# Two-layer graph network on one core: keys from seven block products, squares in two halves at the end of the aggregate, statistics a slot later

## Chip, core and metric

The kernel runs on one core of a Trainium2 chip. The metric is the device time of one launch in microseconds; lower is better. The core has five engines that run side by side and are held together by semaphores: TensorE (PE, matrix products; its weight loads are listed as PEld), VectorE (DVE), ScalarE (ACT), GpSimd (POOL) and SyncE (SP, which here only issues transfers). Transfers are carried by 16 DMA engines. Products land in PSUM, in banks of 128 x 512 numbers; everything else lives in SBUF. All numbers are float32.

## What is computed

There are B = 16 graphs of N = 1024 nodes with C = 256 features, one weighted adjacency matrix for all, and two layers, each with a layer norm and a relu in front and a residual behind:

```python
h = jnp.maximum(_layernorm(x, axis=-1), 0.0)
x = x + L0(h)          # attention, queries from the graph
h = jnp.maximum(_layernorm(x, axis=-1), 0.0)
x = x + L1(h)          # graph convolution, two dense layers with batch norm

# L0
fea = jnp.transpose(x, (0, 2, 1))
c_adj = jnp.mean(fea, axis=1)
diff = c_adj[:, None, :] - c_adj[:, :, None]
A = jnp.abs(jnp.abs(jax.nn.sigmoid(diff) - 0.5) - 0.5) * 2.0
A_s = (A + jnp.transpose(A, (0, 2, 1))) * 0.5
Wg = adj[None, :, :] * A_s
g = jax.nn.relu(jnp.einsum('bcn,bnm->bcm', fea, Wg) * para.reshape(1, C, N))
q = ...                                   # g, split into 4 heads of 64
kv = (x @ kv_w) ...                       # keys and values, 4 heads each
attn = jax.nn.softmax(jnp.einsum('bhnd,bhmd->bhnm', q, k) * scale, axis=-1)
out = jnp.einsum('bhnm,bhmd->bhnd', attn, v)

# L1
deg = row sums + column sums - diagonal of (adj + I)
A_hat = A_norm * dinv[:, None] * dinv[None, :]
agg = jnp.einsum('nm,bmd->bnd', A_hat, features)
h = jax.nn.relu(_batchnorm(agg.reshape(-1, d) @ W1.T + b1, g1, be1))
out = _batchnorm(h @ W2.T + b2, g2, be2)
```

The batch norms of L1 run over all graphs and nodes, so that the kernel has two stages: everything up to the first dense layer, graph by graph (`layers`), and then the second dense layer (`second`), which the change leaves alone.

## The kernel before

**The loop.** `attention` (L1215) walks 16 graphs x 4 units x 4 = 256 steps. A unit is one pair of heads and one half of the queries. In each step TensorE makes two score tiles (`scores`, L1056; ScalarE takes the exponential into a tile `p`, L1064) and two products of the earlier step's `p` with the values (L1099). VectorE adds the `p` tiles up for the softmax's denominators (L1085, L1088). The tiles `p` have four buffers.

**The background.** Between the scores and the next step, the step takes work from a generator `background(b)`, which holds all other products: each piece is worth some microseconds (`yield 1.71` for two products, `yield 0.86` for one), and a step takes pieces until the sum is at `due`, which grows evenly to `total` over a graph's 16 steps (L1231 to L1236). Instructions are issued to each engine in just the order in which this Python code makes them, and engines work their own list from front to back. `soon(action)` puts an action off to the beginning of the next piece; `weave(main, (start, side), ...)` takes one piece of each side along with each piece of main from number `start` on.

In the background of graph b stand, in this order:
- four pieces of `keys_values(b+1)`: the keys (L670). Each key block of 128 x 512 is the sum of two products of a weight block of `kvw` with a block of the transposed features `ht`: eight products, copied out of PSUM by ScalarE (L681);
- `queries(b+1)`, 7 x 4 products instead of 8 x 4, by the same way of combining quarters (Strassen and Winograd's) that the change now uses for the keys. VectorE weighs adjacency tiles for it (`weigh`, L493) and combines them (`take`, L569);
- the other four pieces of `keys_values(b+1)`, the values, with the second half of `normed(b-1)`, the layer norm for layer 1;
- `aggregate(b-1)`: 7 x 4 products (`pa`), in 14 pieces; from the fourth piece on `summed(b+2)` goes along, the first layer norm of graph b+2 and `differences(b+2)`, which sends the node means through HBM to every partition (`cbc`);
- `prepare(b+2, hidden(b-1))`: the 14 products of the first dense layer (`py`), with `squares(b+2)` after the second product and `gathered(b+2, k)` after the seventh and the tenth.

Graph 0 has a background of its own, with `plain_queries(1)`, the adjacency's combination for the aggregates (`graph`) and the degrees.

**Squares.** The transposed features `ht` come by way of HBM: `squares` (L432) turns 32 x 32 blocks on VectorE into one tile `sq` of 1 MB (tag `h`, a pool with two buffers) and GpSimd issues one transfer to `hsq_d`; `gathered` brings it back in the other order, in four transfers for each half, issued by SP.

```python
sq = p2.tile([P, CC, N], F32, tag="h", name=f"sq_{b}")
for k in range(CC):
    nc.vector.transpose(...)
nc.gpsimd.dma_start(out=hsq_d[b], in_=sq)
```

**Banks.** `bank(name)` hands out the three PSUM banks of the pool `ps_mm` in turn, to `pg`, `pk`, `pv`, `pa`, `py` and `sums` alike: a product can start when the third one before it in this series has been emptied.

**Hidden.** In `hidden` (L795) seven products a half give four blocks, `m1` to `m7`. `m1` and `m5` are emptied by ScalarE (L831, L851), the others by additions on VectorE: `m2` L837, `m3` L842, `m4` L847, `m6` L860, `m7` L866. `put` (L822) has GpSimd send the block to HBM (L824) and puts the batch norm's statistics of the block (L825, VectorE) off with one `soon`. The order of products is m1, m5, m6, m2, m3, m7, m4 in the first half and m1, m6, m2, m5, m7, m3, m4 in the second.

**Other lines.** `steps_of` (L780): the differences of the aggregate's blocks (L786, L787 on VectorE, L788 on GpSimd). L727 and L744: the aggregate's last additions and scaling. `fold` (L1134, L1135): a unit's denominators. `load_later` (L303): loads `w1`, makes its combinations on GpSimd and spreads `dinv` over the partitions.

Of the kernel before, what the change touches and what calls it, by code (L numbers as in the profile page):

```python
# [10 lines left out]
F32 = mybir.dt.float32  # L11
# [6 lines left out]
P = 128  # L18
# [5 lines left out]
def gnn_two_layers_kernel(  # L24
# [12 lines left out]
    nc = tc.nc  # L37
    B, N, C = x.shape
# [60 lines left out]
    def layers(shifted):  # L99
# [31 lines left out]
        def soon(action):  # L131

            queue.append(action)
# [169 lines left out]
        def load_later():  # L303
            later["w1"] = big.tile([P, CC, H1], F32, tag="w1", name="w1")
            nc.sync.dma_start(out=later["w1"], in_=w1_t.rearrange("(k p) j -> p k j", p=P))
            later["s"] = big.tile([P, 4, H1 // 2], F32, name="w1s")
            s1, s2, s3, s4 = (later["s"][:, i] for i in range(4))
            a11, a12, a21, a22 = w1_quarters()
# [123 lines left out]
        def squares(b):  # L432

            sq = p2.tile([P, CC, N], F32, tag="h", name=f"sq_{b}")
            for k in range(CC):
                nc.vector.transpose(
                    sq[:, k].rearrange("p (i t s) -> p i t s", i=NS, s=SQ),
                    hs["a", b][:, :, k * P : (k + 1) * P].rearrange("p t (i s) -> p i t s", s=SQ),  # L440
                )
            nc.gpsimd.dma_start(out=hsq_d[b], in_=sq)

        def gathered(b, k):

# [222 lines left out]
                        yield 1.71  # L668

        def keys_values(b):  # L670
            ht = hts[b]
            ks[b] = [p4.tile([P, N], F32, tag="k", name=f"k_{b}_{k}") for k in range(CC)]
            for g in range(NH):
                for j in range(CC):
                    cols = slice(g * FB, (g + 1) * FB)
                    pk = bank(f"pk_{b}_{j}_{g}")
                    for k in range(CC):
                        product(
                            pk, kvw[:, k, j * P : (j + 1) * P], ht[k][:, cols], k == 0, k == CC - 1
                        )  # L680
                    nc.scalar.copy(ks[b][j][:, cols], pk)  # L681
                    yield 1.71

            vs[b] = [p4.tile([P, NT, P], F32, tag="v", name=f"v_{b}_{k}") for k in range(CC)]
            for g in range(NT // 2):
                pv = bank(f"pv_{b}_{g}").rearrange("p (j c) -> p j c", j=2)
# [10 lines left out]
                for k in range(CC):  # L697
                    nc.scalar.copy(
                        vs[b][k][:, 2 * g : 2 * g + 2, :], pv[:, :, k * P : (k + 1) * P]
                    )  # L700
                yield 1.71

        def aggregate(b):
# [91 lines left out]
        def hidden(b):  # L795
# [26 lines left out]
            def put(y, n, j):  # L822
                i = b * NH + n
                nc.gpsimd.dma_start(out=y1_d[i][:, j, :], in_=y)  # L824
                soon(lambda: nc.vector.bn_stats(stats1[:, j, i, :], y))  # L825

            add = nc.vector.tensor_add

# [97 lines left out]
        def summed(b):  # L926
            yield from Norm(b, True).all()
            differences(b)
            yield 0.0

        def prepare(b, products):


            w = weighers[b]
            yield from islice(products, 1)
            yield from islice(products, 1)
            squares(b)
            yield from weave(islice(products, 5), (0, islice(w, 2)))
            gathered(b, 0)
            yield from weave(islice(products, 3), (0, islice(w, 1)))  # L940
            gathered(b, 1)
            yield from weave(islice(products, 3), (0, islice(w, AHEAD - 3)))
            yield from products
# [3 lines left out]
        def background(b):  # L947

            if b == 0:
                differences(1)  # L950
                for k in range(CC):
# [263 lines left out]
        def attention():  # L1215
# [7 lines left out]
            for s in range(len(steps) + 2):  # L1223
                if s < len(steps):
                    unit, g = steps[s]
                    b = unit.at[0]
                    if s % per_graph == 0:
# [460 lines left out]
```

## Time and profile before

| what | us |
| --- | --- |
| median of 3 runs (lowest, highest) | 2484.15 (2481.71, 2485.78) |
| the profiled execution | 2482.2 |
| its span in the trace | 2480.3 |
| first score product | 54.1 |
| start of graph 1, 2, 3 | 164.9, 303.7, 439.9 |
| each of the graphs 3 to 13 | 135.47 or 135.48 |
| graph 14 | 122.2 |
| last graph from | 2052.3 |

Times in the text are microseconds from the beginning of the span. From the beginning of the last graph 428 us are left, of which the second stage has the larger part. In the lists of waits a line gives the engine that stood, the tile and line that it was about to do, what released it, then the sum of the waits, their number and the longest. In timelines a line gives start, duration, engine, line, operation, tiles out and in, and sizes.

### The profile page before, as it was taken

The page shows a single profiled execution, that of the slowest core. Times are in us where ns is not written, and L with a number is a line of the kernel's source. Part 1 is how long each engine was busy: PE and PEld are TensorE (multiplying, and loading weights), DVE is VectorE, ACT ScalarE, POOL GpSimd, SP SyncE. Part 2 cuts the span into 40 slices and gives each one's busy share as a digit, 9 for nine tenths or more (in the row PEclk, how much of TensorE's full clock was granted, in tenths as well). Part 3 has the DMA queues.
Part 4 walks back from the last instruction along what each step waited for, and adds up shares of the span by engine and source line. Part 5 has one row for each costly group of instructions (what it writes and reads, how often), then busy time and mean ns, then how long its engine had stood idle before and what let it go on. Part 6 is the DMA issues. An engine that isn't in the chain of part 4 may idle for free. (4 is left out here: it accounts for less than half of the span.)

```text
span 2480.3 us, 35952 instructions
## 1 busy us (share of the span) xinstructions
PE 2418.3 (97%) x13290; PEld 829.3 (33%) x13290; DVE 1999.8 (81%) x3103; ACT 1261.2 (51%) x1870; POOL 565.2 (23%) x632
## 2 busy tenths in 40 slices
PE   9999999999999999999999999999999999999995
PEld 4333232332323232323323232323233232334444
DVE  5678887979798888889797978888897978767775
ACT  7764454545463645545454645355454534345554
POOL 1480202112121202021111212120201102136652
PEclk9999999999999999999999999999999999999997
DMA  4665535354555544453545555544535453456559
GB/s 145 198 218 175 181 124 191 120 198 157 181 174 191 168 168 162 144 181 118 210 143 175 170 191 170 187 160 148 177 126 197 133 199 122 157 205 222 192 198 373
DMA packets 202682, 437.19 MB, mean 176 GB/s; under 512 B 21248, under 2 KB 96512, under 8 KB 196736
## 3 DMA queue, kind: packets, MB, share of 16 engines
q1 hardware_dynamic: 173328, 327.29, 39.9%
q0 software_dynamic: 29168, 107.50, 11.4%
q8 instruction: 107, 1.75, 0.3%
q14 instruction: 79, 0.65, 0.1%
HBM read 331.36 MB, written 103.35 MB: 175 GB/s over the span
## 5 line engine op out<-in xcount | busy, mean ns | idle before, releaser
L1064 ACT ACTIVATE p<-sc 128x1024 f32<-128x1024 f32 x512 | 495.6, 1020 | 581.4 <-PE sc L1056 579.7
L1088 DVE TENSOR_TENSOR acc<-acc,p 128x1024 f32<-128x1024 f32 x384 | 469.5, 1223 | 81.6 <-ACT p L1064 60.3
L1056 PE MATMUL sc<-q,k 64*64 64x512 f32 x4096 | 500.1, 603 | 4.2 <-ACT p L1064 4.2
L1099 PE MATMUL o<-p,v 128*64 128x512 f32 x2048 | 494.6, 604 | 0.0
L174 PE MATMUL pa<-aht,h_b 128*64 128x512 f32 x1536 | 346.0, 592 | 1.1 <-ACT h_b L368 1.1
L174 PE MATMUL pg<-w,x_h 128*64 128x512 f32 x1472 | 332.0, 592 | 1.9 <-DVE x_h L579 1.9
L1056 PEld LDWEIGHTS sc<-q,k 64*64 64x64 f32 x4096 | 131.7, 132 | 340.9 <-issue 287.8
L1117 POOL DMA_DIRECT2D out_d<-os x58 | 33.9, 584 | 914.9 <-DVE os L1113 883.9
L1099 PEld LDWEIGHTS o<-p,v 128*64 128x64 f32 x2048 | 124.4, 136 | 297.9 <-issue 272.4
L493 DVE SCALAR_TENSOR_TENSOR w<-w,adj 128x1024 f32<-128x1024 f32 x128 | 166.2, 1306 | 31.9 <-ACT w L514 26.1
L174 PEld LDWEIGHTS pa<-aht,h_b 128*64 128x64 f32 x1536 | 110.0, 137 | 220.7 <-issue 208.8
L174 PEld LDWEIGHTS pg<-w,x_h 128*64 128x64 f32 x1472 | 105.6, 137 | 212.4 <-issue 201.0
L506 ACT ACTIVATE w<-cbc,csum 128x512 f32<-128x512 f32 x256 | 170.3, 716 | 4.7 <-DMA cbc<-csum_d 4.7
L514 ACT ACTIVATE w<-w 128x1024 f32<-128x1024 f32 x128 | 135.5, 1059 | 2.5
L569 DVE TENSOR_TENSOR w<-w,w 128x1024 f32<-128x1024 f32 x112 | 133.2, 1219 | 1.5
L174 PE MATMUL py<-at,w1s 128*64 128x512 f32 x448 | 109.5, 598 | 9.7 <-DVE y L837 7.5
L174 PE MATMUL pv<-kvw_f,ht 128*64 128x256 f32 x1024 | 116.1, 379 | 0.0
L174 PE MATMUL pk<-ht,kvw_f 128*64 128x512 f32 x512 | 115.2, 592 | 0.2 <-ACT ht L430 0.2
L174 PE MATMUL py<-at,w 128*64 128x512 f32 x464 | 113.3, 595 | 1.3 <-DVE at L727 0.7
L368 ACT ACTIVATE x_h<-x_h,lnsm_a 128x256 f32<-128x256 f32 x120 | 70.5, 593 | 74.6 <-DMA aht<-aht_d 67.1
L1085 DVE TENSOR_TENSOR acc<-p,p 128x1024 f32<-128x1024 f32 x64 | 79.2, 1237 | 31.5 <-ACT p L1064 31.5
L1428 ACT ACTIVATE yin_f<-yin_f,sm_f 128x512 f32<-128x512 f32 x128 | 93.5, 802 | 15.0 <-DMA yin_f<-y_d 14.9
(197 smaller groups left out, 2967.1 us busy)
## 6 DMA issues: line engine op xcount, KB each, us to landing
aht<-aht_d SPq DMA_DIRECT2D x224, 512.0 KB
adj<-in_adj_dram SPq DMA_DIRECT2D x128, 512.0 KB
y_d<-y POOLq DMA_DIRECT2D x128, 256.0 KB, 3.8
yin_f<-y_d SPq DMA_DIRECT2D x32, 1024.0 KB
para<-in_para_dram SPq DMA_DIRECT2D x64, 256.0 KB
x_d<-x_x POOLq DMA_DIRECT2D x16, 1024.0 KB, 5.1
xo_f<-x_d SPq DMA_DIRECT2D x32, 512.0 KB
out_dram<-xo_f POOLq DMA_DIRECT2D x32, 512.0 KB, 11.1
```

The lines of the kernel that those rows point to most:

```text
L174: nc.tensor.matmul(dst[r], left[:, r], right, start=start, stop=stop)
L368: nc.scalar.activation(self.h[:, t, :], self.src[:, t, :], AF.Relu, bias=self.sm[:, 1, t : t + 1], scale=self.sm[:, 0, t : t + 1], accum_o ...
L493: nc.vector.scalar_tensor_tensor(w, w, 1.0, a, op0=ALU.add, op1=ALU.mult)
L506: nc.scalar.activation(w[:, t, :].rearrange("p (t q) -> p t q", q=P), cbc[:, q * NT // NH : (q + 1) * NT // NH], AF.Abs, bias=csum[:, th * ...
L514: nc.scalar.activation(made[i], made[i], AF.Tanh, scale=-0.5 / C)
L569: nc.vector.tensor_sub(block(i)[part], block(x)[part], block(y)[part])
L1056: nc.tensor.matmul(sc[part, e, :], ks[b][k][r, m * P + c * HW : m * P + (c + 1) * HW], qs[b][k][r, f * FB : (f + 1) * FB], start=True, sto ...
L1064: nc.scalar.activation(pr, sc, AF.Exp)
L1085: nc.vector.tensor_add(self.acc, self.held, pr)
L1088: nc.vector.tensor_add(self.acc, self.acc, pr)
L1099: nc.tensor.matmul(self.o[r, :], vs[b][k][:, m, r], pr[:, e, :], start=(m == 0), stop=(m == NT - 1),)
L1428: nc.scalar.activation(y, y, AF.Relu, bias=sh[:, j : j + 1], scale=scale[:, j : j + 1])
```

## The change

The diff, without the parts that only move lines; `key_steps`, `keys_of` and `values_of` are new.

```diff
@@ load_later
+            later["kvs"] = kvs = p1.tile([P, 4, P], F32, tag="kvs", name=f"kvs_{kind}")
+            combined(kvs, key_weights())
             later["s"] = big.tile([P, 4, H1 // 2], F32, name="w1s")
+            combined(later["s"], w1_quarters())
@@ squares
-            sq = p2.tile([P, CC, N], F32, tag="h", name=f"sq_{b}")
             for k in range(CC):
+                sq = p1.tile([P, N], F32, tag="sq", name=f"sq_{b}_{k}")
                 nc.vector.transpose(
...
-            nc.gpsimd.dma_start(out=hsq_d[b], in_=sq)
+                nc.gpsimd.dma_start(out=hsq_d[b][:, k], in_=sq)
+                yield 0.0
@@ keys_values
+            if b > 2:
+                yield from values_of(b)
+                yield from keys_of(b)
+                return
...
+        def key_steps(b):
+            b11, b12, _, b22 = blocks(hts[b])
+            two = p1.tile([P, N], F32, tag="sq", name=f"kt_{b}")
+            t1, t2 = steps[b] = two[:, :FB], two[:, FB:]
+            nc.vector.tensor_sub(t1, b12, b11)
+            nc.vector.tensor_sub(t2, b22, t1)
+
+        def keys_of(b):
...
+            def second(m):
+                add(c11, m, c12)
+                sub(b21, b21, t2)
+
+            def fifth(m):
+                add(c21, m, c12)
+                nc.gpsimd.tensor_add(c12, c12, c22)
+                nc.gpsimd.tensor_add(c22, c22, c21)
+
+            for i, (left, right, after) in enumerate(
+                (
+                    (a11, b11, lambda m: nc.scalar.copy(c12, m)),
+                    (a12, b21, second),
+                    (s1, t1, lambda m: nc.scalar.copy(c22, m)),
+                    (s2, t2, lambda m: add(c12, m, c12)),
+                    (s3, b12, fifth),
+                    (s4, b22, lambda m: add(c12, m, c12)),
+                    (a22, b21, lambda m: add(c21, m, c21)),
+                )
+            ):
+                made = bank(f"pk_{b}_{i}")
+                product(made, left, right, True, True)
+                after(made)
+                yield 0.86
+
+        def values_of(b):
+            ht = hts[b]
+            if b > 2:
+                key_steps(b)
...
+                if b > 2 and g == NT // 2 - 1:
+                    _, b12, _, b22 = blocks(ht)
+                    soon(lambda: nc.vector.tensor_sub(b12, b22, b12))
@@ hidden, put
-                soon(lambda: nc.vector.bn_stats(stats1[:, j, i, :], y))
+                soon(lambda: soon(lambda: nc.vector.bn_stats(stats1[:, j, i, :], y)))
@@ summed
             differences(b)
             yield 0.0
+            yield from squares(b)
@@ prepare
-            squares(b)
-            yield from weave(islice(products, 5), (0, islice(w, 2)))
             gathered(b, 0)
+            yield from weave(islice(products, 6), (0, islice(w, 2)))
@@ background, graph 0
-                yield from weave(
-                    plain_queries(1), (0, w), (4, norm), (5, graph()), (7, degrees())
-                )
+                asked, build, sums = plain_queries(1), graph(), degrees()
+                yield from weave(
+                    islice(asked, 13),
+                    (0, w),
+                    (4, norm),
+                    (5, islice(build, 8)),
+                    (7, islice(sums, 6)),
+                )
                 differences(2)
+                yield from weave(asked, (0, build), (0, sums))
@@ background, the others
                 yield from weave(islice(products, 4), (0, islice(w, 4)))
+                yield from weave(queries(b + 1), (0, double(w)), (9, islice(norm, 5)))
                 if b == 1:
                     load_later()
-                yield from weave(queries(b + 1), (0, double(w)), (9, islice(norm, 5)))
@@ attention
-                        total -= 10.3 * (b == B - 1)
+                        total -= 10.3 * (b == B - 1) + 0.8 * (1 < b < B - 1)
```

`combined` holds the four combinations (s1 = a21 + a22, s2 = s1 - a11, s3 = a11 - a21, s4 = a12 - s2) that stood in `load_later`. In what is computed nothing changes but the order of additions in the keys of graphs 3 to 15. For these graphs the values now come first, in the place of the keys, and the keys follow behind the queries. The pool p1 has one buffer for each tag, so that the two halves of `sq` and the keys' two differences take turns in one buffer of 512 KB.

More of the change, by code (lines that the diff above doesn't have):

```diff
@@ L305, in load_later, with combined @@
             nc.sync.dma_start(out=later["w1"], in_=w1_t.rearrange("(k p) j -> p k j", p=P))
+            later["kvs"] = kvs = p1.tile([P, 4, P], F32, tag="kvs", name=f"kvs_{kind}")
+            combined(kvs, key_weights())
             later["s"] = big.tile([P, 4, H1 // 2], F32, name="w1s")
-            s1, s2, s3, s4 = (later["s"][:, i] for i in range(4))
-            a11, a12, a21, a22 = w1_quarters()
+            combined(later["s"], w1_quarters())
+        def combined(into, quarters):
+            s1, s2, s3, s4 = (into[:, i] for i in range(4))
+            a11, a12, a21, a22 = quarters
             nc.gpsimd.tensor_add(s1, a21, a22)
@@ L432, in squares @@
         def squares(b):
-            sq = p2.tile([P, CC, N], F32, tag="h", name=f"sq_{b}")
             for k in range(CC):
+                sq = p1.tile([P, N], F32, tag="sq", name=f"sq_{b}_{k}")
                 nc.vector.transpose(
-                    sq[:, k].rearrange("p (i t s) -> p i t s", i=NS, s=SQ),
+                    sq.rearrange("p (i t s) -> p i t s", i=NS, s=SQ),
                     hs["a", b][:, :, k * P : (k + 1) * P].rearrange("p t (i s) -> p i t s", s=SQ),
                 )
-            nc.gpsimd.dma_start(out=hsq_d[b], in_=sq)
+                nc.gpsimd.dma_start(out=hsq_d[b][:, k], in_=sq)
+                yield 0.0
         def gathered(b, k):
@@ L682, in keys_values, with blocks, key_weights @@
                     yield 1.71
+            yield from values_of(b)
+        def blocks(pair):
+            return [pair[k][:, g * FB : (g + 1) * FB] for k in range(CC) for g in range(NH)]
+        def key_weights():
+            return [kvw[:, k, j * P : (j + 1) * P] for j in range(CC) for k in range(CC)]
+        def key_steps(b):
[5 more added lines that the diff above has]
+        def keys_of(b):
+            ks[b] = [p4.tile([P, N], F32, tag="k", name=f"k_{b}_{k}") for k in range(CC)]
+            a11, a12, _, a22 = key_weights()
+            s1, s2, s3, s4 = (later["kvs"][:, i] for i in range(4))
+            b11, b12, b21, b22 = blocks(hts[b])
+            c11, c12, c21, c22 = blocks(ks[b])
+            t1, t2 = steps.pop(b)
+            add, sub = nc.vector.tensor_add, nc.vector.tensor_sub
+            def second(m):
[24 more added lines that the diff above has]
+                key_steps(b)
             vs[b] = [p4.tile([P, NT, P], F32, tag="v", name=f"v_{b}_{k}") for k in range(CC)]
```

## The prediction

> **What bounds the kernel now.** I read the page first, then the table of windows over the whole span, then who waits for whom on TensorE, then one graph in the middle (graph 8, 1117.24 to 1252.71 us) engine by engine. The chain that ended last tells little here: it is cut at 2210 us, in the second layer's normalisation, which the change doesn't touch.
>
> ```profile
> span 2480.3 us, 35952 instructions
> ...
> PE 2418.3 (97%) x13290; PEld 829.3 (33%) x13290; DVE 1999.8 (81%) x3103; ACT 1261.2 (51%) x1870; POOL 565.2 (23%) x632
> ```
>
> TensorE is busy for 97% of the span. Busy is modelled, so I checked the pace: in the timeline one 128x128 by 128x512 product follows the next after 0.86 us (31.76 to 32.62), at a granted clock of 1.00, and from graph 3 to 13 every graph takes 135.47 us. What TensorE waits for in the whole middle (210 to 2050 us):
>
> ```profile
> PE py L174 <- DVE y L837: 7.5, 13, 0.6
> PE py L174 <- DVE y_sum L866: 2.2, 13, 0.2
> PE py L174 <- DVE y L842: 0.5, 1, 0.5
> ```
>
> So 0.74 us a graph, all in the hidden products, whose three PSUM banks VectorE must empty. And before that, in the beginning (60 to 210 us):
>
> ```profile
> PE sc L1056 <- ACT p L1064: 3.7, 1, 3.7
> PE pg L174 <- DVE x_h L579: 1.9, 1, 1.9
> ```
>
> A graph has 16 steps (two score tiles, two value products, some background). VectorE, by step of graph 8 (columns: length, PE, PEld, DVE, ACT, POOL, clock, DMA share, GB/s), shown for steps 5, 7, 12, 13 and 14:
>
> ```profile
> 1160.12:1169.01 8.89, 8.89 (x50) 2.71 (x49) 8.75 (x15) 1.94 (x2) 0.28 (x1) 1.00 0.41 145
> ...
> 1176.20:1185.12 8.92, 8.92 (x74) 4.44 (x72) 5.59 (x8) 6.79 (x15) 0.00 (x0) 1.00 0.95 343
> ...
> 1219.22:1226.40 7.18, 7.18 (x43) 2.15 (x41) 5.00 (x9) 1.94 (x2) 0.62 (x1) 1.00 0.09 36
> 1226.40:1235.29 8.89, 8.89 (x50) 2.72 (x48) 8.18 (x10) 4.22 (x6) 3.00 (x2) 1.00 0.56 174
> 1235.29:1243.77 8.48, 8.31 (x47) 2.26 (x45) 8.24 (x12) 4.24 (x6) 3.82 (x5) 1.00 0.64 221
> ...
> sum 135.47, PE 134.73 PEld 43.17 DVE 115.35 ACT 68.44 POOL 23.32; mean PE 8.42 PEld 2.70 DVE 7.21 ACT 4.28 POOL 1.46
> ```
>
> VectorE is full in steps 13 to 15 and 3 to 6, and has room in 7 to 12. Its late point is step 14:
>
> ```profile
> 1226.98 0.69 DVE L787 TENSOR_TENSOR at<-at,at 128x512 f32<-128x512 f32 x1
> 1227.59 0.70 DVE L1134 STREAM_TRANSPOSE acc<-acc 128x512 f32<-128x512 f32 x1
> ...
> 1233.31 2.37 DVE L438 STREAM_TRANSPOSE sq<-x_h 128x1024 f32<-128x1024 f32 x2
> ...
> 1238.31 2.54 DVE L1088 TENSOR_TENSOR acc<-acc,p 128x1024 f32<-128x1024 f32 x2
> 1240.77 0.69 DVE L842 TENSOR_TENSOR y<-py,y 128x512 f32<-128x512 f32 x1
> ```
>
> L842 (m3) empties a bank that m1 of the second half, three products on, needs; that product is due at 1241.73, the bank is free at 1241.46. So VectorE may be 0.3 us later here before TensorE stands. Behind L842, L866 (m7) must end by 1242.59 for the product after; it ends at 1242.70, and that is the 0.17 us of the list above.
>
> **What the Trainium skill says.** "PSUM — Partial Sum Buffer", "Engine vs sequencer instructions": VectorE's and GpSimd's queues are strictly first in, first out. The trace agrees: VectorE stood 4.75 us for an adj load at 191.7 with nothing passing it. "DMA: Bandwidth & Descriptors", "Anatomy of one DMA": a GpSimd transfer costs some 2.0 us plus bytes/436 GB/s until its semaphore fires. The trace: out_d, 256 KB, 2.4 us (page's rule 2.6); hsq_d, 1 MB, 4.2 at least and 5.0 in the median (rule 4.4). It agrees where nothing else is in flight.
>
> **The change part by part.** Times are graph 8's, with 11 dropped (28.81 is 1228.81); the order is that of the changed program's instructions on each engine.
>
> *One product less.* Keys of graphs 3 to 15 take 7 products in place of 8: 13 x 0.86 = -11.2 us. ACT loses two copies (0.585 us each) a graph, which nothing waits for.
>
> *The keys' differences.* VectorE gets nine operations of 0.69 us: two in step 0, one in step 1, two in step 6, four in step 7. Steps 1 and 2 have 2.0 us of VectorE's idling (0.16, 0.39, 1.47), which hides nearly all of the 2.1 us there. In steps 6 and 7 I walked VectorE's new order: the sums of step 7 are due at 80.75 instead of 79.49, end at 83.2, and the add that empties the fourth key bank ends at 83.9, while the seventh product wants that bank at 83.49. Stall: 0.45 us (bounds 0 and 0.9, as ScalarE's eight value copies at 0.377 in steps 0 and 1 replace four of 0.585). The following add waits for GpSimd (c12+c22; like operations took 1.29 to 1.71 us), twice, some 2.5 us; that falls into the 5.3 us that VectorE stood at 81 to 87 and reaches no one.
>
> *Squares.* The two transposes (1.22 us each) leave step 13 for step 12, and go from one buffer of 1 MB in p2 to a single buffer of 512 KB in p1, used twice. So the second transpose waits until the first one's transfer has landed; the built program has this wait on VectorE. In graphs 2 to 13 the order there becomes: L787, first square, the two at-operations of the seventh aggregate product, second square, fold, the sums of step 13, two hidden adds, fold, the sums of step 14, L842. Walk: first square ends at 28.81; GpSimd is free then (its b12 subtraction runs 27.10 to 28.81) and issues at 29.05; VectorE stands before the second square at 30.09. With a landing time L it goes on at 29.05+L+0.05, a hole h = L-0.99. Nothing behind it idles, so h arrives whole at L842's successor: without a hole it would end at 40.92, with one at 40.92+h, and TensorE needs it at 41.73. TensorE's stall there is h-0.76 instead of 0.17. In step 15 the same lag makes the old 0.57 into 0.68. Together h-0.82 more than before.
>
> L is not shown for 512 KB. From below: the rule's 2.0+1.2 = 3.2 us (an estimate; between out_d's 2.4 and hsq_d's 4.2 the line gives 3.0). From above: 5.0, the median of the whole 1 MB. The broadcast of cbc (512 KB, issued at 28.70) flows in the same microseconds; I take 4.0. Then h = 3.0 and the cost is 2.2 us a graph (1.4 to 3.2).
>
> In graph 1 a step's border stands between the two squares, fold and sums fill the hole: nothing lost, perhaps 0.4 us won. Graph 14 has no squares: it keeps its 0.86.
>
> *Statistics one slot later.* The 0.69 us of L825 go behind L866 and L842, which is in the walk above; without the hole this and the earlier squares would end the 0.17 and most of the 0.57.
>
> *Loads.* gathered(b,0) is issued earlier, so SP stands for its landing ahead of two adj loads; their first user (w in step 14) is 8 us later. gathered(b,1) comes one product later, 10 us before its first reader. Neither is on the path.
>
> *The beginning.* differences(2) goes three background slots ahead: the cbc load that ScalarE stood 4.7 us for at 143.6 lands earlier, and TensorE's 3.7 goes. load_later moves behind the queries: SP stood from 173.6 to 188.0 over w1 and dinv ahead of the adj loads, VectorE 4.75 and TensorE 1.9. Both go: -5.7 us (0 to -5.7). What load_later now delays (aht for 240 us, dbc) has 10 us. What is late next is not seen.
>
> *Sum.* Graphs 2 to 13: -0.86+0.45+2.2 = +1.8, times 12 = +21.5. Graph 14 -0.9, graph 1 -0.4, beginning -5.7. In all +14.5. The profiled execution took 2482.2 us (span 2480.3), so 2496.7; its median is 2484.15, 2.0 above, so **2498**.
>
> **The rivals.**
> - *The wait is covered* (faster). L is 2.2 us or less, as out_d's 2.4 nearly is, or the copy out is let go earlier than I think. Then 13 products (-11.2), the beginning (-5.7), 0.45 x 12 = +5.4 and some -0.3 x 12 = -4: 2469. For: without other traffic small transfers land fast. Against: the skill's 3.2 and hsq_d's own minimum. The point at which the whole change turns is L = 2.8: 12 x (L-2.22) = 7.0. Chance 0.18.
> - *It comes out even.* L between 2.6 and 3.0, or no stall among the keys and L near 3.2: 2484. For: the estimate's low end is close by. Against: cbc's transfer. 0.11.
> - *VectorE becomes the bound* (slower still). It goes from 115.35 to 121.6 us of some 135, 90%; if a third of the 6.2 reaches TensorE on top of the hole, 12 x 2.1 = +25: 2523. For: L842's margin of 0.3 us. Against: 20 us idle a graph, most of it just behind the keys. 0.07.
> - *The forecast*, the hole in steps 12 to 15: its own range 2487 (L 3.2, no key stall) to 2511 (L 5). 0.64.
>
> **How the numbers follow.** A difference of 0.2%, 5 us, is what can be told from no change. Slower: 0.64 x 0.97 + 0.07 = 0.69; the even case and a rest of the forecast give same 0.12; faster 0.19. The range of 8 in 10 goes from 2472, well into the faster case, to 2513.
>
> **What would show it.** Right: VectorE idle 2 to 4 us before the second sq transpose in graphs 2 to 13, ended by hsq_d's landing; TensorE waiting 1.5 to 3.5 us in py for the add of L842; graphs 2 to 13 at some 137.3 us. The keys: a wait of 0 to 0.9 us in pk. The beginning: no gap over 1 us between 140 and 210. Wrong: a graph of 134 us, hsq_d landing under 2.8 us, or fold standing between the squares in the trace.

## The result and the profile after

The changed kernel took 2587.98 us (median of 4 runs, 2584.95 to 2594.78) beside 2483.32 us of the kernel before (4 runs, 2481.71 to 2485.78): ratio 1.0424, 95% interval 1.0404 to 1.0443. It is slower, as forecast, but by 105 us, not by 14. The page of its profiled execution begins:

```profile
span 2586.0 us, 36047 instructions
...
PE 2438.8 (94%) x13238; PEld 827.1 (32%) x13238; DVE 2080.3 (80%) x3220; ACT 1244.1 (48%) x1844; POOL 599.7 (23%) x675
```

TensorE has 52 matmul records fewer (13 products of four) and is "busy" 20 us longer, and its share fell from 97% to 94%. So two things happened: it stood more, and it was slower while it was busy. What it stood for from graph 1 to 14 (210 to 2140 us; columns: sum, number, longest):

```profile
PE py L174 <- DVE y L913: 37.9, 13, 3.2
PE pa L174 <- DMA aht<-aht_d: 20.4, 1, 20.4
PE pk L174 <- ACT k L735: 15.4, 12, 1.3
PE py L174 <- DVE y L931: 10.8, 11, 1.6
PE pk L174 <- DVE k L723: 8.3, 12, 1.1
PE pk L174 <- DVE k L736: 5.8, 8, 0.7
PE py L174 <- DVE y L908: 1.8, 2, 1.2
```

L913, L931 and L908 are the hidden additions that were L842, L860 and L837 before. Three groups stand here: one wait of 20.4 us for the aggregate's first block, some 2.5 us a graph among the keys (pk), some 4 us a graph in the hidden products (py). Between 60 and 210 us the same list is empty: the 3.7 and 1.9 us of the beginning are gone.

By the first score product of each graph, and over graphs 2 to 13 (mean of a graph, from the trace; "half clock" is the time with a granted clock of 0.5, which costs half of itself):

| us | before | after |
| --- | --- | --- |
| graph 0 | 110.8 | 105.5 |
| graph 1 | 138.8 | 160.0 |
| graphs 2 to 13, each | 135.53 | 143.02 |
| of it TensorE idle in py / pk | 0.79 / 0 | 4.07 / 2.46 |
| of it half clock | 0 | 4.27 |
| graph 14 | 122.23 | 121.93 |

The 105.7 us between the spans are thus -5.2 in graph 0, +21.2 in graph 1, +89.9 in graphs 2 to 13 and -0.3 in graph 14.

**Graph 1.** SyncE's issues in the timeline of the changed kernel (start, duration, queue, line, tiles):

```profile
219.51 0.46 SPq L320 DMA_DIRECT2D dinv_d<-deg  x1
230.57 0.34 SPq L321 DMA_DIRECT2D dbc_f<-dinv_d  x1
235.84 0.36 SPq L320 DMA_DIRECT2D dinv_d<-deg  x1
246.64 0.34 SPq L321 DMA_DIRECT2D dbc_f<-dinv_d  x1
247.08 2.59 SPq L785 DMA_DIRECT2D aht<-aht_d  x5
```

The store of dinv and the load of dbc run twice. They stand at the end of the new helper `combined`, which is called once for the keys' weights and once for w1; the description of `combined` above names only its four combinations. Each pass holds SyncE for about 11 us until its store has landed, the second store waits 4.8 us for the first load besides, and the five loads of aht queue behind both. From 236.5 to 257.0 us the granted clock is 0.5; TensorE works 4.2 us of that, which costs 2.1 us on top of the wait.

**Graph 8, the squares.** VectorE's timeline (idle time before an instruction, and what ended it, in brackets), with GpSimd's and TensorE's below it:

```profile
1288.97 1.24 DVE L444 STREAM_TRANSPOSE sq<-x_h 128x1024 f32<-128x1024 f32 x1
...
1290.82 0.69 DVE L798 TENSOR_TENSOR at<-at,dbc_f 128x512 f32<-128x512 f32 x1
1295.66 1.25 DVE L444 STREAM_TRANSPOSE sq<-x_h 128x1024 f32<-128x1024 f32 x1 [4.16 <-DMA hsq_d<-sq]
...
1298.14 3.32 DVE L1165 TENSOR_TENSOR acc<-acc,p 128x1024 f32<-128x1024 f32 x2
...
1306.57 0.68 DVE L913 TENSOR_TENSOR y<-py,y 128x512 f32<-128x512 f32 x1
```

```profile
1290.50 0.56 POOL L448 DMA_DIRECT2D hsq_d<-sq  x1 [0.31 <-DVE sq L444]
1297.21 0.53 POOL L448 DMA_DIRECT2D hsq_d<-sq  x1 [6.14 <-DVE sq L444]
1297.76 1.28 POOL L877 TENSOR_TENSOR at<-at,at 128x512 f32<-128x512 f32 x1
```

```profile
1307.31 1.08 PE L174 MATMUL py<-at,w 128*64 128x512 f32 x4 [3.17 <-DVE y L913]
```

The first store, issued at 1290.50, lets the buffer go at 1295.6, and VectorE stands 4.16 us with the second transpose at its head. Then the pair of sums of exponentials takes 3.32 us instead of 2.54, beside GpSimd's subtraction at 1297.76, which itself waited behind the second store. TensorE stands at 1302.20 (0.85) and before 1307.31 (3.17).

**The clock.** Four stretches of 3.41 us around that place; two are shown (columns: stretch, length, PE, PEld, DVE, ACT, POOL, granted clock, DMA share, GB/s):

```profile
1304.88:1308.29 3.41, 0.98 (x6) 0.41 (x8) 3.31 (x5) 0.00 (x0) 0.72 (x2) 1.00 0.72 217
1308.29:1311.70 3.41, 3.41 (x14) 0.65 (x14) 3.41 (x6) 1.91 (x3) 2.21 (x3) 0.50 0.43 160
```

TensorE works 0.98 of 3.41 us, and the next 3.41 us are granted half the clock: 14 matmul records where the stretch after it holds 28. Such a stretch counts as busy and appears in no list of waits. Graphs 2 to 13 have 15 of them; before they had none. Two graphs of the changed kernel show the price: graph 3 has none of them, 5.5 us of idle time, and takes 140.0 us; graph 7 has two, 6.1 us of idle time, and takes 143.7.

### The profile page after: what moved, and what is told of

It reads as the page before. It is cut to its first block, busy times and chain, and to the rows that moved or that the text cites. A ratio compares the mean times of both kernels' runs of the same rounds, so it can differ in the third digit from the quotient of the medians.

```text
span 2586.0 us, 36047 instructions
## 1 busy us (share of the span) xinstructions
PE 2438.8 (94%) x13238; PEld 827.1 (32%) x13238; DVE 2080.3 (80%) x3220; ACT 1244.1 (48%) x1844; POOL 599.7 (23%) x675
## 5 line engine op out<-in xcount | busy, mean ns | idle before, releaser
L1165 DVE TENSOR_TENSOR acc<-acc,p 128x1024 f32<-128x1024 f32 x384 | 479.7, 1249 | 67.5 <-ACT p L1141 46.5
L174 PE MATMUL pa<-aht,h_b 128*64 128x512 f32 x1536 | 346.1, 595 | 21.8 <-DMA aht<-aht_d 20.4
L174 PEld LDWEIGHTS pg<-w,x_h 128*64 128x64 f32 x1472 | 105.7, 137 | 204.6 <-issue 191.1
L174 PE MATMUL py<-at,w 128*64 128x512 f32 x464 | 119.8, 614 | 38.6 <-DVE y L913 37.9
L174 PE MATMUL py<-at,w1s 128*64 128x512 f32 x448 | 118.3, 639 | 12.6 <-DVE y L931 10.8
L564 ACT ACTIVATE q<-q 128x512 f32<-128x512 f32 x56 | 34.9, 630 | 134.4 <-DVE q L562 134.2
L895 POOL DMA_DIRECT2D y_d<-y x112 | 61.7, 552 | 150.6 <-DVE y L908 84.8
```

The lines of the kernel that those rows point to most:

```text
L174: nc.tensor.matmul(dst[r], left[:, r], right, start=start, stop=stop)
L1165: nc.vector.tensor_add(self.acc, self.acc, pr)
```

## The experiments

All stand on `dbc_once`, the changed kernel with the doubled lines made single, so that graph 1 disturbs the rest less. Those of part 4, and `pool_dbc`, stand on `old_squares`, which has the squares of the kernel before as well; `start_only` has its keys too.

**1. The doubled store: dbc_once and dbc_early**

```diff
@@ load_later
             combined(later["s"], w1_quarters())
+            later["dbc"] = const.tile([P, N], F32, tag="dbc", name=f"dbc_{kind}")
+            nc.sync.dma_start(out=dinv_d.rearrange("(t p) -> p t", p=P), in_=dinv)
+            nc.sync.dma_start(
+                out=later["dbc"], in_=dinv_d.rearrange("(o n) -> o n", o=1).to_broadcast([P, N])
+            )
@@ combined: the same three statements taken out
```

> The changed kernel with one edit: the store of dinv and the broadcast load of dbc stand once, at the end of load_later, and no longer in `combined`, which is called twice. Theory: graph 1's one wait of 20.4 us for the first block of aht is SyncE's two passes of store and load (its aht loads leave at 247 us, with one pass they could leave at about 231), so the time falls by about 16 us, to about 2572, and a wait of 4 to 5 us stays there; graphs 2 to 13 stay at 143 us each. Rival: the wait is that of load_later's place behind the queries, whose w1 load and GpSimd steps come late anyway; then less than 5 us come back (2583 or more).

Measured: 2575.19 us, 1.0375 (1.0352 to 1.0398). Graph 1 fell from 160.0 to 145.5, the wait from 20.4 to 5.2 us, as the theory had it; the span is 16.2 us shorter, the median 12.8.

dbc_early also calls load_later ahead of the queries (one line moved).

> As dbc_once, and load_later stands ahead of the queries again, as in the kernel before. Theory: the whole 20.4 us of graph 1 are gone, at most 2 us of SyncE's waiting for graph 0's last loads come back: about 2567 to 2569, graph 1 at about 139 to 141 us. Rival: graph 1 is long because of what the differences and the graph's building now do there, not because of load_later: then it stays above 150 us and the time above 2575.

Measured: 2578.74 us, 1.0381 (1.0363 to 1.0398). A miss for both: the aht wait is gone, but graph 1 takes 147.7. SyncE now stands in front of the queries' adjacency loads, for the degrees that the store needs (L311) and then for the store's landing (L312),

```profile
SPq L312 <- DMA dinv_d<-deg: 7.8, 1, 7.8
SPq L311 <- POOL deg L97: 7.1, 1, 7.1
```

and TensorE waits 5.5 us behind VectorE, which stands 7.6 us for one of these loads. At both places tried on SyncE's queue, the pair holds up something.

**2. Squares or keys: old_squares and old_keys**

```diff
@@ old_squares: squares
-            for k in range(CC):
-                sq = p1.tile([P, N], F32, tag="sq", name=f"sq_{b}_{k}")
+            sq = p2.tile([P, CC, N], F32, tag="h", name=f"sq_{b}")
+            for k in range(CC):
...
+            nc.gpsimd.dma_start(out=hsq_d[b], in_=sq)
@@ old_squares: summed, prepare
-            yield from squares(b)
+            squares(b)
+            yield from weave(islice(products, 5), (0, islice(w, 2)))
             gathered(b, 0)
-            yield from weave(islice(products, 6), (0, islice(w, 2)))
@@ old_keys: keys_values, attention
-            if b > 2:
-                yield from values_of(b)
-                yield from keys_of(b)
-                return
...
-                        total -= 10.3 * (b == B - 1) + 0.8 * (1 < b < B - 1)
+                        total -= 10.3 * (b == B - 1)
```

> As dbc_once, with the squares as the kernel before makes them (one tile of 1 MB out of the pool of two buffers, its store one transfer, behind the second product of the linear layer's stretch). Theory: VectorE's wait of 4.2 us for the single buffer goes, with it TensorE's wait of 4.0 us and 1.7 us of half clock behind it: about 5 us a graph, 60 us in all less than dbc_once (about 2512), a graph at about 138 us; the records of a granted clock of 0.5 fall from three a graph or so to those of the kernel before. Rival: VectorE has too much to do in a graph; then the two transposes are only late elsewhere and less than 2 us a graph come back (2548 or more).

Measured: 2512.56 us, 1.0125 (1.0109 to 1.0142): the theory's 2512. A graph takes 137.83, TensorE's idle time in py is 0.65 us (0.79 before the change), and half clock fell from 3.98 to 0.57 us.

> As dbc_once, with the keys as the kernel before makes them (eight products of whole blocks ahead of the values, no differences, no kvs). Theory: in graphs 2 to 13 the keys' three waits (0.6, 1.3 and 0.7 us) go, and the product that they saved (0.86) comes back: 1.7 us a graph, about 20 us in all less than dbc_once; the wait of 4.0 us at the squares stays, and with it the half clock behind it; a graph takes about 141.5 us. Rival: VectorE is what bounds these graphs (80% of the span): then the waits at the keys come back at another place when they go here, and taking VectorE's keys' work away (about 6 us a graph) shortens a graph by 4 us or more, the wait at the squares shrinking too.

Measured: 2497.75 us, 1.0068 (1.0051 to 1.0085). The theory missed: taking the keys back was worth 77 us, though the squares still have one buffer. The rival's numbers came true (a graph is 6.2 us shorter, 4 or more were forecast, and the wait at the squares shrank); whether its reason did, VectorE's load, this run alone can't tell. VectorE's wait for hsq_d, 49.8 us in dbc_once, is not among the longest any more, and there is no half clock in graphs 2 to 13. The order of the instructions shows why: with four pieces of 1.71 us and no 0.8 in the pacing sum, a step ends between the two transposes, and the fold and sums of the next step stand between them. The keys' part alone costs 2.3 us a graph (old_squares against before), the squares' alone 1.1 (old_keys), both together 7.3 (dbc_once). So the rest, 3.9 us, needs both: either VectorE is short of time, or the order has been shifted.

**3. The order alone: pace and apart**

```diff
@@ pace: attention
-                        total -= 10.3 * (b == B - 1) + 0.8 * (1 < b < B - 1)
+                        total -= 10.3 * (b == B - 1) + 1.2 * (1 < b < B - 1)
@@ apart: squares takes the blocks to do
-            for k in range(CC):
+            for k in ks:
@@ apart: summed
-            yield from squares(b)
+            yield from squares(b, (0,))
@@ apart: prepare
+            for _ in squares(b, (1,)):
+                pass
             gathered(b, 0)
```

> dbc_once with one constant changed: the sum that paces the background work is cut by 1.2 instead of 0.8 in graphs 2 to 13. Nothing is added or taken away; in the built order VectorE's four instructions of the next step (fold and two sums of exponentials) now stand between the two transposes of the squares, as they do in old_keys. Theory: the hole is made by both transposes standing in one step with one buffer, which is what the keys' seven shorter pieces did to the pacing; now the first store lands behind other work, VectorE's 50 us of waiting for hsq_d, TensorE's 3.2 us in one piece and the half clock go, while the keys' 2.6 us a graph and about 1 us behind the second transpose stay: a graph at 138.5 to 139.5 us, 2520 to 2532 in all. Rival: it is the keys' extra work on VectorE that makes the squares late; then the order of these few instructions matters less than 1 us a graph and the time stays above 2560.

Measured: 2532.84 us, 1.0208 (1.0191 to 1.0225): 42 us less by one constant, with the same instructions. TensorE's idle time in py fell from 4.17 to 1.87 us a graph, half clock from 3.98 to 1.71. In graph 8 the fold and the two sums now stand between the transposes, and the second one waits:

```profile
1267.65 1.25 DVE L444 STREAM_TRANSPOSE sq<-x_h 128x1024 f32<-128x1024 f32 x1 [0.47 <-DMA hsq_d<-sq]
```

The hole is a matter of order, not of VectorE's load. No run gave the squares two buffers in the new place. The forecast's upper end was passed by a microsecond.

> dbc_once with the second transpose and its store moved to the place where the squares stood before (behind two products of the linear layer); the first stays at the aggregate's end, still with one buffer. Theory: the same hole is gone by another way, the buffer is free long before the second transpose, and no product waits behind it there: VectorE's wait for hsq_d under 1 us a graph, a graph at about 137.5 to 138.5 us as in old_squares, 2512 to 2525 in all. Rival: a transpose of 1.24 us in that place makes its own wait of 2 us or more at the linear layer's products; then 2535 or more.

Measured: 2526.5 us, 1.0184 (1.0167 to 1.0201), 1.5 us above the range. No wait for hsq_d is among VectorE's longest. But

```profile
PE py L174 <- DVE y L908: 19.2, 13, 2.4
```

where old_squares has 7.8 us for the same addition. The first transpose at the aggregate's end, 1.24 us ahead of the fold, sums and additions, costs 0.9 us a graph on its own. old_keys and pace, which have it in the same place, wait 20.8 and 20.2 us for this addition too.

**4. The keys' waits: mixed_keys, late_finish, c22_first, keys_third**

In old_squares, where only the keys are left, VectorE's timeline in the keys of graph 8 is:

```profile
1193.62 0.69 DVE L561 TENSOR_TENSOR q<-q,para 128x512 f32<-128x512 f32 x1 [1.66 <-DMA para<-in_para_dram]
1194.23 0.68 DVE L722 TENSOR_TENSOR k<-pk,k 128x512 f32<-128x512 f32 x1
...
1195.92 2.55 DVE L1164 TENSOR_TENSOR acc<-acc,p 128x1024 f32<-128x1024 f32 x2 [0.41 <-ACT p L1140]
1198.39 0.68 DVE L735 TENSOR_TENSOR k<-pk,k 128x512 f32<-128x512 f32 x1
```

VectorE stood 1.66 us for the last block of para, with the keys' first addition (L722) behind it, and the fourth product's addition (L735) stood behind two sums of exponentials.

```diff
@@ mixed_keys: keys_values
-                yield from values_of(b)
-                yield from keys_of(b)
+                key_steps(b)
+                values, keys = values_of(b), keys_of(b)
+                for one in (values, keys, values, keys, values, keys, values, keys):
+                    yield from islice(one, 1)
+                yield from keys
@@ mixed_keys: values_of
-            if b > 2:
-                key_steps(b)
@@ late_finish: queries, seventh
-                soon(lambda: soon(lambda: finish(1, 0)))
+                later_by(8, lambda: finish(1, 0))
@@ c22_first: late_finish and keys_of
+                    (s1, t1, lambda m: nc.scalar.copy(c22, m)),
                     (a11, b11, lambda m: nc.scalar.copy(c12, m)),
                     (a12, b21, second),
-                    (s1, t1, lambda m: nc.scalar.copy(c22, m)),
@@ keys_third: late_finish, pool_dbc and attention
-                        total -= 10.3 * (b == B - 1) + 0.8 * (1 < b < B - 1)
+                        total -= 10.3 * (b == B - 1) + -0.9 * (1 < b < B - 1)
```

`later_by(n, action)` puts an action off by n pieces, as n nested `soon` do.

> old_squares with the keys' first four products put between the four groups of the values (value, key, value, key and so on, then the last three keys), the same instructions in another order. Theory: the keys' waits (2.5 us a graph in old_squares: 1.3 for ScalarE's copy of c22, 0.7 and 0.5 for VectorE) come from seven products of 0.86 us in a row over three banks, each released by a reader that takes longer; with 1.7 us of values between them they fall under 1 us a graph: a graph at 135.5 to 136.3 us, 2486 to 2498 in all. Rival: they come from what stands ahead on VectorE and ScalarE (the wait for para of 1.4 us, the exponentials) whatever the order; then they only move and the time stays within 8 us of old_squares (2505 or more).

Measured: 2556.21 us, 1.0302 (1.0285 to 1.032), 44 us more than old_squares; neither theory. The waits among the keys shrank to one of 1.9 us, but a larger one came up at a value product:

```profile
PE pv L174 <- DVE q L609: 44.0, 12, 4.0
PE pk L174 <- DVE ht L771: 20.1, 12, 1.9
```

Its bank is that of the queries' last product, which VectorE empties in L609, and L609 has come to stand behind a step's fold and sums:

```profile
1212.64 0.70 DVE L1211 STREAM_TRANSPOSE acc<-acc 128x512 f32<-128x512 f32 x1
1213.38 0.69 DVE L1212 TENSOR_REDUCE part<-acc 128x16 f32<-128x512 f32 x1
1213.98 2.54 DVE L1165 TENSOR_TENSOR acc<-acc,p 128x1024 f32<-128x1024 f32 x2
1216.45 0.68 DVE L609 TENSOR_TENSOR q<-pg,q 128x512 f32<-128x512 f32 x1
```

> old_squares with the last multiplication of the queries (finish(1, 0), which waits for its para block) put off by six more pieces, behind the keys' first products; its result is read only in the next graph. Theory A: VectorE's wait of 1.4 us for para, ahead of the keys' first addition, is the root of the keys' waits: all three (0.5, 1.3 and 0.7 us a graph) shrink, to under 1 us together, a graph at 136 us, about 2495 in all. Theory B: only the first of them hangs on para; the copy of c22 stands behind the exponentials on ScalarE and the fourth product's addition behind the sums of exponentials on VectorE, whatever para does: 1.5 to 2 us a graph stay, 2503 to 2508 in all.

Measured: 2494.77 us, 1.0054 (1.0038 to 1.0069): theory A's time, but not by its way. The wait for para and the first of the three are gone, as B said, and 1.79 us of idle time a graph are left in pk, as B said; the rest of A's gain is that the remaining waits no longer bring half clock (none in graphs 2 to 13, 0.57 us before) and a graph takes 136.62.

> late_finish with the keys' product s1 by t1 taken first instead of third, so that ScalarE's copy of c22 stands ahead of the step's exponentials. Theory B: the wait of 1.3 us for that copy goes too and 0.7 us at most stays: a graph at 135.3 to 136 us, 2485 to 2493 in all; each of the three waits then had its own cause, the order in which readers of three banks come up on engines that have other work. Rival: the keys' chain of additions on VectorE (five of 0.69 us and a subtraction, between sums of exponentials of 1.25 us) sets the pace in any order; then the same time is lost at another of the seven products and the time is that of late_finish within 4 us.

Measured: 2530.95 us, 1.0197 (1.0182 to 1.0213): 36 us more than late_finish, against both. The copy's wait is gone, but the addition of the product now third stands behind the two sums, and these stand 3.24 us for ScalarE's exponentials,

```profile
PE pk L177 <- DVE k L725: 39.9, 12, 3.3
```

and the single wait of 3.3 us brings half clock in 11 of 12 graphs.

> late_finish with GpSimd's queue for dinv and dbc (as in pool_dbc) and the pacing sum raised by 0.9 instead of cut by 0.8 in graphs 2 to 13, so that the step's scores, exponentials and sums stand behind the keys' third product instead of the second; ScalarE's copy of c22 then comes ahead of the exponentials. GpSimd's queue is worth about 8 us of it (2486 without any other gain). Theory A: the two waits left at the keys (1.06 us for the copy of c22, 0.73 us for the fourth product's addition) have causes of their own, so the first goes and a graph is at 135.5 us: 2472 to 2477. Theory B: both are one chain, from the step's scores over two exponentials and two sums of exponentials to the fourth product's addition, and the copy's wait only spends a part of it earlier; then the wait for the addition grows to 1.5 us or more and a graph stays at 136.3 to 136.8 us: 2484 to 2489.

Measured: 2508.82 us, 1.0108 (1.0091 to 1.0125): neither. The scores moved by one product, as meant, but the step before moved too, and its fold and sums came to stand ahead of L612, the queries' last addition, as in mixed_keys:

```profile
PE pk L177 <- DVE q L612: 32.0, 12, 3.0
```

Every arrangement waits at a place of its own behind the same kind of block. In mixed_keys and keys_third it is a fold and the two sums of exponentials, 3.9 us of VectorE's time; in old_squares, late_finish and c22_first the two sums alone, 2.5 us, which first stand for ScalarE's exponentials (0.41, 1.56 and 3.24 us in graph 8). Of the steps of 7 to 9 us three in four have two sums and half have a fold, and whatever addition stands behind them holds its bank that long. Three banks of 0.86 us don't cover it. An order in which seven products in a row pass free of a wait was not found.

**5. What beats both: pool_dbc and start_only**

```diff
@@ pool_dbc: mixed_keys and load_later
-            nc.sync.dma_start(out=dinv_d.rearrange("(t p) -> p t", p=P), in_=dinv)
-            nc.sync.dma_start(
+            nc.gpsimd.dma_start(out=dinv_d.rearrange("(t p) -> p t", p=P), in_=dinv)
+            nc.gpsimd.dma_start(
                 out=later["dbc"], in_=dinv_d.rearrange("(o n) -> o n", o=1).to_broadcast([P, N])
```

> mixed_keys with the store of dinv and the load of dbc issued by GpSimd's queue instead of SyncE's. Theory: graph 1's wait of 5.4 us for aht and its 3.4 us of cost in half clock come from SyncE holding the aht loads behind the store of dinv (about 8 to 11 us to land); GpSimd has nothing urgent there, so graph 1 falls from 144.6 to about 137 to 139 us and the time by 6 to 8 us against mixed_keys. Rival: dbc itself then comes late for the aggregate's first scaling and TensorE waits for it instead; then less than 2 us come back.

Measured: 2547.73 us, 1.0268 (1.0251 to 1.0285), 8.5 us less than mixed_keys, as the theory had it and half a microsecond more; graph 1 takes 136.3 us, and TensorE waits neither for aht nor for dbc (VectorE stands 1.0 us for dbc).

start_only is that, with keys (as in old_keys) and squares (as in old_squares) as before.

> The kernel before with the change's beginning and later statistics alone: graph 0 woven as in the changed kernel, differences(2) ahead of the queries' end, load_later behind the queries, keys and squares as before, and the store of dinv and the load of dbc on GpSimd's queue as in pool_dbc. Theory: graph 0 keeps its 5.2 us, graph 1 is at 136.3 us as in pool_dbc instead of 138.8, graphs 2 to 14 at 135.5 us as before: 7 to 9 us less than before, 2472 to 2476, ratio 0.996 to 0.9975. Rival: the later statistics or the differences' earlier loads cost something in every graph that the keys and squares hid; then the ratio is 0.999 or more.

Measured: 2469.27 us (5 runs, 2469.16 to 2469.79) against 2480.84, ratio 0.9951 (0.9937 to 0.9964): faster than both kernels, by 0.5% against the one before, and more than expected. All that TensorE waits for from 60 to 2120 us (L896 is m2's addition there, L837 in the kernel before):

```profile
PE py L174 <- DVE y L896: 8.2, 13, 1.0
```

Graph 0 gives 5.2 us, graph 1 2.5, and graphs 2 to 13 0.39 each, where only the later statistics differ from before. That last part I had expected at nothing. The waits for L866 are gone (0.17 us a graph); the other 0.2 us are not explained.

**The sum over all kernels.** Mean graph of 2 to 13, from the traces. The last column is 135.53, plus TensorE's idle time less before's 0.79, less 0.86 where the keys have seven products, plus half of the half clock:

| us | idle | half clock | graph | worked out |
| --- | --- | --- | --- | --- |
| changed kernel | 6.53 | 4.27 | 143.02 | 142.54 |
| dbc_once | 6.48 | 3.98 | 142.88 | 142.35 |
| dbc_early | 7.04 | 3.41 | 143.26 | 142.62 |
| old_keys | 1.97 | 0 | 136.65 | 136.71 |
| old_squares | 3.16 | 0.57 | 137.83 | 137.32 |
| pace | 4.29 | 1.71 | 139.61 | 139.02 |
| apart | 4.06 | 1.71 | 139.16 | 138.79 |
| mixed_keys | 6.00 | 3.98 | 141.89 | 141.87 |
| pool_dbc | 6.04 | 3.70 | 141.84 | 141.77 |
| late_finish | 2.44 | 0 | 136.62 | 136.32 |
| c22_first | 4.06 | 3.13 | 139.67 | 139.51 |
| keys_third | 3.39 | 1.99 | 138.40 | 138.27 |
| start_only | 0.63 | 0 | 135.14 | 135.37 |

Three terms explain every kernel to 0.65 us a graph; what is left over, from -0.23 to 0.64, is open.

## Why the prediction was wrong

The direction held, and the squares' hole came where the prediction put it. The size failed: the sum on record was +14.5 us, the spans differ by 105.7, and four fifths of the miss come from three things that the sum had at little or nothing, namely the keys' waits, the transfers of load_later and half clock.

- *One product less*, -0.86 a graph: right. Graph 14, which has no squares, shows it bare in late_finish (121.37 against 122.23); in the changed kernel the keys' waits leave 0.3 of it.
- *The squares' hole*: the walk was right, down to "L842's successor" (L913), and the formula too: idle time 4.16 plus the 0.78 that the sums took longer, less 0.76, is 4.18; TensorE stood 0.85 and 3.17, 4.02. The term that failed is L, taken at 4.0: the 26 stores of 512 KB took 3.6 to 6.7 us to land, 5.2 in the median, above even the bound of 5.0. The estimate from the Trainium skill, "DMA: Bandwidth & Descriptors" ("Anatomy of one DMA"), was 3.2. Graph 8's store flies beside the load of cbc and two adj loads, 512 KB each; that this traffic makes the difference was not tested. The kernel before gave a hint that was not used: there y_d's stores of 256 KB took 3.8 us in the median, and the prediction drew its lower line through out_d's 2.4. The 0.78 us by which the sums were longer was not in the sum either. Together py rose by 3.3 us, not 2.2: 13 us in twelve graphs. That there would be a hole at all hung on where the pacing put the step's end (pace); the prediction had this right because it read the order of the instructions and not only the diff.
- *The keys' differences*, "Stall: 0.45 us": 2.46 measured, 24 us more in all. The walk had only VectorE's sums in it. It left out that VectorE stands for the last block of para, with the keys' first addition behind it (19.4 us in 12 graphs; in the kernel before once in these graphs, 1.6 us), and that ScalarE's copy of c22 stands behind two exponentials (late_finish took the first away, c22_first the second).
- *"What load_later now delays (aht for 240 us, dbc) has 10 us"*: 20.4 us of wait and 2.1 of half clock; graph 1 is longer by 21.2 instead of shorter by 2.3 (the 0.4, and the wait of 1.9 at 199.8 us, which lies in graph 1). I moved load_later in thought as it stood before and didn't count its DMAs anew: the store and the load had become two of each, and aht comes behind them on SyncE's queue. Even one pass was too much: by the prediction's own reading SyncE stood over load_later for 14.4 us (173.6 to 188.0), and dbc_once still waits 5.2 us.
- *Half clock* has no term in the sum: 15 stretches of 3.41 us in graphs 2 to 13 cost 25.6 us.
- *The beginning*: both waits are gone. Graph 0, where only the 3.7 us were forecast, gave 5.2: 1.7 us of it is a stretch of half clock that had followed that wait. The 1.9 us of graph 1 can be seen in pool_dbc and start_only, where graph 1 takes 136.3 us beside 138.8 before.

In all 13 us for the hole, 24 for the keys, 22 for graphs 0 and 1 and 26 for half clock; graph 14 adds 0.6, and some 6 us of the miss of 91 (0.48 a graph) stay without a cause. The rival "VectorE becomes the bound" lay nearer in time (2523), but its reason is not what happened: in pace VectorE does all of the work, 42 us faster. Two sums on record are off: 2496.7 and 2.0 make 2498.7, and L at 3.2 without a key stall gives 2484, as the even rival has it, not the 2487 of the forecast's own range.

## What to carry over

A stall that is taken into a sum has a second price when TensorE's clock follows its work: ask how much idle time a few microseconds hold, not only how long the wait is, and look for half clock inside "busy". Where one buffer is used twice, the landing time measured at that place decides, and whether a step's other work stands between the two uses; one constant of the pacing may decide that for both. When a block of code is moved or made into a helper, count its DMAs per call and follow each on its queue.

## What the runs showed of the hardware

**Half clock comes on a fixed grid.** In each trace all stretches of a granted clock of 0.5 begin on one grid of 3.413 us, to 0.004 us, in graphs whose length is no multiple of it. Twelve traces have such a stretch after the first graph and before 2130 us. Their cells of this grid that ran at full clock and held over 0.3 us of TensorE's idle time are 523. Of the cells with under 1.81 us of it none was followed by a half-clock cell, of those over 2.02 us all were (106 in all were followed). The other two traces, before and start_only, have no cell over 1.6 us of idle time there and no half clock. So the same wait of 3.17 us costs 1.7 us more or nothing, by its place. Here is one that the grid cuts in two, in dbc_early:

```profile
1008.37:1011.79 3.42, 1.62 (x8) 0.29 (x4) 3.28 (x5) 0.00 (x0) 1.47 (x2) 1.00 1.11 287
1011.79:1015.20 3.41, 2.05 (x12) 0.66 (x16) 3.41 (x6) 0.92 (x2) 1.78 (x2) 1.00 0.58 217
1015.20:1018.61 3.41, 3.41 (x28) 1.08 (x26) 3.38 (x7) 2.91 (x4) 1.14 (x3) 1.00 0.43 159
```

TensorE worked 1.62 and 2.05 us in the two cells, idle 1.8 and 1.4, and the third keeps its full clock. Several short waits in one cell add up: behind two key waits within 3 us (0.58 and 1.29 us in one graph) the changed kernel has half clock four times. The Trainium skill, "TensorE: Matmul & The Clock Gate", "What's actually happening", says that the window is free-running and 3413 ns long, which these traces show, and that the clock falls after an idle window; here a window didn't have to be idle throughout, 1.8 to 2.0 us of idle time were enough.

**A store in pieces of 4 bytes.** dinv, 4 KB, held SyncE 10.4 us until it had landed, twice as long as 512 KB of hsq_d. The skill, "DMA: Bandwidth & Descriptors", "Rules for kernel authors", says that a last dimension that isn't contiguous becomes one descriptor per element. The trace agrees: it has over a thousand packets of 4 bytes. But they are not where the time goes. All of them lie within a microsecond and are over at 222.7 us, the landing is reported from 228.2 to 230.4, and between the two the trace has no packet of data. What fills this time is open, and no run here stored dinv in another form.

**Two engines at SBUF.** VectorE's pair of sums took 3.32 instead of 2.54 us beside GpSimd's subtraction of 1.28 us. The skill, "SBUF — State Buffer", "SBUF: two separate sides", has the two share a pair of ports that one of them holds for a whole instruction; the sums overlap the subtraction for 0.90 us (1298.14 to 1299.04), and the loss is 0.78. In the changed kernel's trace up to 2100 us, none of the 374 single sums (128x1024) without GpSimd's arithmetic beside them took more than 1.23 us, and all 22 that took over 1.45 had some beside them. No run took the subtraction away alone.
